# Two groups of edges a step, offsets read four at a time, and one-hot products with the table standing still

## The chip, the cores and the metric

The kernel runs on one core of one Trainium2 chip. A core has five engines with queues of their own: PE (TensorE, matrix products into PSUM), DVE (VectorE), ACT (ScalarE), POOL (GpSimd) and SP (SyncE, which here only issues transfers). The metric is device microseconds of one execution, the median of several runs.

## The reference, cut to what matters

There are 12,500 nodes with 48 features and 200,000 edges, sorted by destination. Two graph layers follow each other, and each ends in a residual sum and a layer norm:

```
x1  = layernorm(x  + segment_sum(relu([x[dst], x[src], e32] @ W1 + b1) @ W2 + b2, dst))
out = layernorm(x1 + (1 + eps) * x1 + segment_sum(relu(x1[src] + e48), dst))
```

W1 is 128 by 128 (48 rows for x[dst], 48 for x[src], 32 for the edge features), W2 is 128 by 48. All is float32. The sources are random, so x[src] and x1[src] are gathers of rows from all over the table. The destinations are sorted, so a run of 512 edges touches only a narrow window of destinations.

## The kernel before, in words

**Groups.** The edges are padded and cut into 391 groups of 512, each of four tiles of 128 edges (`TPC`, `NCHUNK`, lines 43 to 46). The nodes are cut into 14 segments of 7 blocks of 128. The destinations of a group lie in a window of 48 nodes, whose start is worked out on the chip (`base`, `off`, lines 208 to 222). `rel` holds each edge's destination less the window's start. A check on the chip (`check_windows`) lets a general path run instead if an edge falls outside; with these inputs it does not run.

**Layer 0, one group a step.** `fetch0` (399) issues four indirect DMAs on POOL, one for each tile, each gathering 128 rows of 48 values into the tile `cat`. `fill0` (404) copies the edge features into `cat` on ACT, writes the one-hot of the destination within the window on DVE, reads the group's offset into a register of SP, and lets SP load 48 rows of the projected table (`a_dram`) into one of four weight tiles `wcat`. `turn0` (414) transposes the four tiles on PE and DVE copies them to `cat_t`. `hidden0` (422) multiplies by `wcat` on PE, and ACT applies bias and relu. `message0` (429) multiplies by W2, and DVE adds b2. `sum0` (439) sums the messages by window on PE with the one-hot, and `add_window` (309) reads the offset into a register of DVE and adds the 48 by 48 result into the segment's sum.

**The order** is written out by hand (`manual_schedule`). `run` (443) goes over steps k and calls, in the order of its list, each stage for the group k less its distance: in layer 0 the fetch five groups ahead, the fill two ahead, then sum (three behind), message (two behind), hidden (one behind) and turn. Every engine works through its own instructions in this order. `finish0` (362) takes each segment's sums to x1 when its last group is through, writes x1 to HBM (`x1_dram`) and keeps x1 in SBUF as three bf16 pieces (`xp`). `project` (263) makes the table that `wcat` is loaded from.

**Layer 1.** `fetch1` (480) gathers rows of `x1_dram`, `fill1` makes the one-hot, `message1` (492) adds edge features on DVE and applies relu on ACT, and `sum1` sums as in layer 0. For 28 of the 391 groups (`PE_GROUPS`, every 13th from the 26th) no gather is issued. Their rows come from `products` (546), in batches of two groups: `place` (509) writes where in its block each source lies and turns that over on PE; for each of the 98 blocks of x1, `select` (523) makes a one-hot of 128 by 1024 on DVE in bf16, and `multiply` (528) multiplies it with the block's three pieces on PE, adding in PSUM. The one-hot stands in PE as the weight (a load for each of 8 tiles) and the pieces pass (144 columns). A `tensor_reduce` then adds the three pieces. `products` is a generator: `lead1` (580) takes one part of it, four blocks, in each step.

Of the kernel before, what the change touches and what calls it, by code (L numbers as in the profile page):

```python
# [55 lines left out]
AHEAD = 5  # L56
NW = 4
EC = 5
FIRST = 26
EVERY = 13  # L60
NPE = 28
BATCH = 2
PIECES = 3
BPS = 4

PE_GROUPS = [FIRST + EVERY * i for i in range(NPE)]
assert PE_GROUPS[-1] < NCHUNK and NPE % BATCH == 0

assert NSEG * NB == NT
STEP = CHUNK * N // E  # L70
STEP4 = 4 * CHUNK * N // E

# [56 lines left out]
def windowed(ctx, tc, dram, flag, x, src, dst, e32, e48, w1, b1, w2, b2, eps, out):  # L129
    nc = tc.nc  # L130
    const = ctx.enter_context(tc.tile_pool(name="const", bufs=1))
    onehots = ctx.enter_context(tc.tile_pool(name="onehots", bufs=2 * BPS))
    cats = ctx.enter_context(tc.tile_pool(name="cats", bufs=AHEAD + 5))
# [3 lines left out]
    node = ctx.enter_context(tc.tile_pool(name="node", bufs=2))  # L137
    psum = ctx.enter_context(tc.tile_pool(name="psum", bufs=1, space=bass.MemoryType.PSUM))
# [4 lines left out]
    dst_i = const.tile([P, NCHUNK * TPC], I32, name="dst_i")  # L143
    nc.sync.dma_start(src_i, src)
    nc.scalar.dma_start(dst_i, dst)
    seg = ctx.enter_context(tc.tile_pool(name="seg", bufs=3))
# [39 lines left out]
    lows = const.tile([1, NCHUNK], F32, name="lows")  # L186
    highs = const.tile([1, NCHUNK], F32, name="highs")
    starts = const.tile([1, NCHUNK], F32, name="starts")
    quads = -(-NCHUNK // 4)
    shares = const.tile([1, quads, 4], F32, name="shares")  # L190
# [9 lines left out]
    def gather(t, table, g, j):  # L200
# [9 lines left out]
    base = const.tile([1, NCHUNK], F32, name="base")  # L210
# [8 lines left out]
    off = const.tile([1, NCHUNK], I32, name="off")  # L219
    nc.vector.tensor_tensor(  # L220
        off, base, starts, op=ALU.subtract
# [6 lines left out]
    )  # L228

# [15 lines left out]
    part = const.tile([P, NPE, TPC], F32, name="part")  # L245
    block = const.tile([P, NPE, TPC], F32, name="block")

    def split_src():
        first = FIRST * TPC
        some = src_i[:, first : first + (NPE - 1) * EVERY * TPC].rearrange(  # L250
            "p (i c) -> p i c", c=EVERY * TPC
        )[:, :, 0:TPC]
        last = src_i[:, PE_GROUPS[-1] * TPC : (PE_GROUPS[-1] + 1) * TPC]
        bits = node.tile([P, NPE, TPC], I32, name="bits")
        for op, by, plus, to in (
            (ALU.bitwise_and, Q - 1, 0.0, part), (ALU.logical_shift_right, 7, 1.0, block)
        ):
            nc.vector.tensor_scalar(bits[:, : NPE - 1, :], some, by, None, op0=op)
            nc.vector.tensor_scalar(bits[:, NPE - 1, :], last, by, None, op0=op)
            nc.vector.tensor_scalar(to, bits, plus, None, op0=ALU.add)  # L260
# [27 lines left out]
    def load_edges(name, table, width, g):  # L288
        c = g // EC
        if g % EC == 0:  # L290
            n = min(EC, NCHUNK - g)
            chunk[name] = echunk.tile([P, EC, TPC * width], F32, name=name)
            nc.sync.dma_start(
                chunk[name][:, :n, :],
                table[g * CHUNK : (g + n) * CHUNK, :].rearrange(
                    "(c p t) d -> p c (t d)", p=P, t=TPC
                ),
            )
        return chunk[name][:, g % EC, :].rearrange("p (t d) -> p t d", t=TPC)

    def one_hot(o, g):
        nc.vector.tensor_tensor(
            o, iota_w[:, None, :].to_broadcast([P, TPC, W]),
            rel[:, g, :, None].to_broadcast([P, TPC, W]), op=ALU.is_equal,
        )

    agg = {}

    def add_window(layer, g, pa):
        s = seg_of(g)  # L310
        if (layer, s) not in agg:
            agg[layer, s] = aggs.tile([D, SROWS], F32, name="agg")
            nc.vector.memset(agg[layer, s], 0.0)
        at = nc.vector.value_load(
            off[0:1, g : g + 1], min_val=low(g) - seg_start(s), max_val=high(g) - seg_start(s)
        )
        cols = agg[layer, s][:, bass.ds(at, W)]
        nc.vector.tensor_tensor(cols, cols, pa, op=ALU.add)  # L318

    def reduce_tiles(hot, msg):  # L320
        pa = psum.tile([D, W], F32, name="pa")
        for j in range(TPC):
            nc.tensor.matmul(pa, msg[:, j, :], hot[:, j, :], start=j == 0, stop=j == TPC - 1)  # L323
# [73 lines left out]
    cat, ph, h, pm, hot = {}, {}, {}, {}, {}  # L397

    def fetch0(g):
        cat[g] = cats.tile([P, TPC, Q], F32, name="cat")  # L400
        for j in range(TPC):
            gather(cat[g][:, j, W : W + D], x, g, j)

    def fill0(g):
        e = load_edges("e32c", e32, DE, g)
        nc.scalar.activation(cat[g][:, :, W + D :], e, AF.Copy)
        one_hot(cat[g][:, :, :W], g)
        s = seg_of(g)
        at = nc.sync.value_load(
            off[0:1, g : g + 1], min_val=low(g) - seg_start(s), max_val=high(g) - seg_start(s)  # L410
        )
        nc.sync.dma_start(wcats[g % NW][0:W, :], a_dram[s][bass.ds(at, W), :])

    def turn0(g):
        pt = psum.tile([Q, TPC, P], F32, name="pt", bufs=2)
        for j in range(TPC):
            nc.tensor.transpose(pt[:, j, :], cat[g][:, j, :], ident[:P, :P])  # L417
        cat_t = work.tile([Q, TPC, P], F32, name="cat_t")
        nc.vector.tensor_copy(cat_t, pt)  # L419
        h[g] = cat_t  # L420

    def hidden0(g):
        ph = psum.tile([HID, TPC, P], F32, name="ph")
        nc.tensor.matmul(ph, wcats[g % NW], h[g], start=True, stop=True)  # L424
        t = work.tile([HID, TPC, P], F32, name="h")
        nc.scalar.activation(t, ph, AF.Relu, bias=b1_sb)  # L426
        h[g] = t

    def message0(g):
        pm = psum.tile([P, TPC, D], F32, name="pm")  # L430
        for j in range(TPC):
            nc.tensor.matmul(pm[:, j, :], h[g][:, j, :], w2_sb, start=True, stop=True)  # L432
        msg = work.tile([P, TPC, D], F32, name="msg")
        nc.vector.tensor_tensor(  # L434
            msg, pm, b2_sb[:, None, :].to_broadcast([P, TPC, D]), op=ALU.add
        )
        h[g] = msg

    def sum0(g):
        pa = reduce_tiles(cat.pop(g)[:, :, :W], h.pop(g))  # L440
        add_window(0, g, pa)

    def run(stages, finish, lead):
# [3 lines left out]
        for k in range(first, NCHUNK + last):  # L447
            for f, d in stages:
                g = k - d
                if 0 <= g < NCHUNK:  # L450
                    f(g)
                    if d == last:
                        for s in finishes.get(g, []):
                            finish(s)
            lead(k)

    def lead0(k):
        for s in range(1, NSEG):
            if k == first_group(s - 1) + 4:
                load_seg(x, s)  # L460
            if k == first_group(s - 1) + 8:
                project(s)
        if k == 14:
            check_windows()
        if k == 16:
            split_src()

    for g in range(AHEAD):
        fetch0(g)
    project(0)  # L470
    run(
        [(lambda g: g >= AHEAD and fetch0(g), -AHEAD), (fill0, -2), (sum0, 3), (message0, 2),
         (hidden0, 1), (turn0, 0)],
        finish0, lead0,
# [5 lines left out]
    def fetch1(g):  # L480
        if g in PE_GROUPS:
            return
        cat[g] = cats.tile([P, TPC, D], F32, name="xs")
        for j in range(TPC):
            gather(cat[g][:, j, :], x1_dram, g, j)

    def fill1(g):
        hot[g] = work.tile([P, TPC, W], F32, name="hot", bufs=4)
        one_hot(hot[g], g)
# [308 lines left out]
```

## Time and profile before

| what | value |
|---|---|
| median of 3 runs | 4900.48 us (4892.4 to 4907.17) |
| profiled execution, its own time | 3846.41 us |
| its span, first to last instruction | 3844.6 us |
| busy PE / PE weight loads | 2856.8 us (74%) / 2210.8 us (58%) |
| busy DVE / ACT / POOL | 1893.4 us (49%) / 564.0 us (15%) / 2887.0 us (75%) |
| mean granted PE clock | 0.787 |
| indirect DMAs on POOL | 1564 in layer 0, 1452 in layer 1 |
| PE matmul records | 23396 |

The profile is of one execution, and its durations belong to the 3846.41 us; the three runs without a profile lie 1054 us higher. Busy time counts work alone: reading registers, waiting for semaphores and issuing DMAs are not in it. "Granted clock" is the share of full speed at which PE ran. In a group's row, the name before the arrow is what is written, those after it what is read, then the shapes, the count, the busy time with the mean of one, and the engine's idle time just before these instructions.

### The profile page before, as it was taken

The page shows a single profiled execution, that of the slowest core. Times are in us where ns is not written, and L with a number is a line of the kernel's source. Part 1 is how long each engine was busy: PE and PEld are TensorE (multiplying, and loading weights), DVE is VectorE, ACT ScalarE, POOL GpSimd, SP SyncE. Part 2 cuts the span into 40 slices and gives each one's busy share as a digit, 9 for nine tenths or more (in the row PEclk, how much of TensorE's full clock was granted, in tenths as well). Part 3 has the DMA queues.
Part 4 walks back from the last instruction along what each step waited for, and adds up shares of the span by engine and source line. Part 5 has one row for each costly group of instructions (what it writes and reads, how often), then busy time and mean ns, then how long its engine had stood idle before and what let it go on. Part 6 is the DMA issues. An engine that isn't in the chain of part 4 may idle for free. (4 is left out here: it accounts for less than half of the span.)

```text
span 3844.6 us, 67581 instructions
## 1 busy us (share of the span) xinstructions
PE 2856.8 (74%) x23396; PEld 2210.8 (58%) x23396; DVE 1893.4 (49%) x4618; ACT 564.0 (15%) x1329; POOL 2887.0 (75%) x3025
## 2 busy tenths in 40 slices
PE   6888788888888888888886767667677676667731
PEld 4555555556555555556565656656566666656631
DVE  3333333333333333333356766767677676767731
ACT  2222212212212212212110000000000000000000
POOL 7777777777777777777767777777777777777776
PEclk9787877787777777777778888878887887888765
DMA  3222222222222222222222221222122222212221
GB/s 71 43 45 49 44 44 47 46 40 49 49 39 49 45 41 47 48 41 46 38 44 39 50 39 37 55 45 43 38 50 43 45 43 50 43 33 55 45 42 28
DMA packets 293005, 171.68 MB, mean 45 GB/s; under 512 B 109664, under 2 KB 292400, under 8 KB 292656
## 3 DMA queue, kind: packets, MB, share of 16 engines
q0 software_dynamic: 96512, 74.31, 13.1%
q1 hardware_dynamic: 179248, 84.31, 8.0%
q10 hardware_dynamic: 16896, 8.69, 0.7%
q8 instruction: 185, 3.03, 0.3%
q14 instruction: 164, 1.34, 0.1%
HBM read 154.45 MB, written 12.62 MB: 43 GB/s over the span
## 5 line engine op out<-in xcount | busy, mean ns | idle before, releaser
L201 POOL DMA_INDIRECT cat<-in_x_dram,src_i x1564 | 1485.1, 950 | 481.0 <-issue 339.5
L201 POOL DMA_INDIRECT xs<-x_dram,src_i x1452 | 1400.0, 964 | 461.0 <-issue 340.7
L530 PEld LDWEIGHTS <-o 128*128 128x128 bf16 x10976 | 853.0, 112 | 22.6 <-DVE o L525 0.6
L525 DVE TENSOR_SCALAR o<-pt 128x1024 bf16<-128x1024 bf16 x1372 | 848.7, 677 | 5.4 <-PE pt L520 5.4
L419 DVE COPY cat_t<-pt 128x512 f32<-128x512 f32 x391 | 270.2, 691 | 897.5 <-PE pt L417 897.5
L323 PE MATMUL pa<-hot,msg 128*48 128x48 f32 x3128 | 255.8, 234 | 561.3 <-ACT msg L497 561.2
L417 PEld LDWEIGHTS pt<-ident,cat 128*128 128x128 f32 x1564 | 265.6, 176 | 632.2 <-DMA cat<-in_x_dram,src_i 365.1
L424 PE MATMUL ph<-cat_t,wcat 128*128 128x512 f32 x782 | 580.3, 833 | 0.8 <-DVE cat_t L419 0.8
L323 PEld LDWEIGHTS pa<-hot,msg 128*48 128x48 f32 x3128 | 202.6, 144 | 642.3 <-ACT msg L497 623.1
L530 PE MATMUL ph<-xp,o 128*128 128x144 bf16 x4116 | 568.5, 256 | 0.0
L417 PE MATMUL pt<-ident,cat 128*128 128x128 f32 x1564 | 389.4, 347 | 237.2 <-DMA cat<-in_x_dram,src_i 233.9
L530 PE MATMUL pm<-xp,o 128*128 128x144 bf16 x4116 | 563.9, 254 | 0.0
L432 PE MATMUL pm<-w_sb,h 128*128 128x48 f32 x3128 | 538.0, 326 | 1.3 <-ACT h L426 1.2
L432 PEld LDWEIGHTS pm<-w_sb,h 128*128 128x128 f32 x3128 | 484.0, 236 | 27.8 <-ACT h L426 2.4
L426 ACT ACTIVATE h<-ph,b_sb 128x512 f32<-128x512 f32 x391 | 268.4, 686 | 1370.1 <-PE ph L424 1355.6
L530 PE MATMUL pt<-xp,o 128*128 128x144 bf16 x2744 | 453.8, 253 | 0.0
L495 DVE TENSOR_TENSOR m<-xs,e48c 128x192 f32<-128x192 f32 x363 | 131.4, 362 | 549.6 <-DMA xs<-x_dram,src_i 549.0
L497 ACT ACTIVATE msg<-m 128x192 f32<-128x192 f32 x391 | 141.8, 363 | 1611.9 <-DVE m L495 1611.9
L323 PE MATMUL pa<-cat,msg 128*48 128x48 f32 x3128 | 260.8, 237 | 33.4 <-DVE msg L434 25.6
L323 PEld LDWEIGHTS pa<-cat,msg 128*48 128x48 f32 x3128 | 207.8, 147 | 112.1 <-issue 52.9
L434 DVE TENSOR_TENSOR msg<-pm,b_sb 128x192 f32<-128x192 f32 x391 | 139.5, 357 | 233.6 <-PE pm L432 231.3
L318 DVE TENSOR_TENSOR agg<-agg,pa 48x48 f32 x782 | 150.3, 192 | 174.0 <-PE pa L323 122.9
(79 smaller groups left out, 1066.8 us busy)
## 6 DMA issues: line engine op xcount, KB each, us to landing
e48c<-in_e_dram SPq DMA_DIRECT2D x78, 480.0 KB
cat<-in_x_dram,src_i POOLq DMA_INDIRECT x1564
e32c<-in_e_dram SPq DMA_DIRECT2D x78, 320.0 KB
xs<-x_dram,src_i POOLq DMA_INDIRECT x1452
wcat<-a SPq DMA_DIRECT2D x391, 24.0 KB
a<-a ACTq DMA_DIRECT2D x14, 256.0 KB
a<-a ACTq DMA_DIRECT2D x14, 192.0 KB
x_seg<-in_x_dram SPq DMA_DIRECT2D x14, 168.0 KB
```

Of the source, the lines that this page charges most:

```text
L201: nc.gpsimd.indirect_dma_start(out=t, out_offset=None, in_=table, in_offset=bass.IndirectOffsetOnAxis(ap=src_i[:, g * TPC + j : g * TPC + ...
L318: nc.vector.tensor_tensor(cols, cols, pa, op=ALU.add)
L323: nc.tensor.matmul(pa, msg[:, j, :], hot[:, j, :], start=j == 0, stop=j == TPC - 1)
L417: nc.tensor.transpose(pt[:, j, :], cat[g][:, j, :], ident[:P, :P])
L419: nc.vector.tensor_copy(cat_t, pt)
L424: nc.tensor.matmul(ph, wcats[g % NW], h[g], start=True, stop=True)
L426: nc.scalar.activation(t, ph, AF.Relu, bias=b1_sb)
L432: nc.tensor.matmul(pm[:, j, :], h[g][:, j, :], w2_sb, start=True, stop=True)
L434: nc.vector.tensor_tensor(msg, pm, b2_sb[:, None, :].to_broadcast([P, TPC, D]), op=ALU.add)
L497: nc.scalar.activation(msg, m, AF.Relu)
L525: nc.vector.tensor_scalar(o, which, float(b + 1), None, op0=ALU.is_equal)
L530: nc.tensor.matmul(ps[k // PER][:, k % PER, :], o[:, k, :], xp[:, b, :, :], start=False, stop=False, skip_group_check=True,)
```

## The change

1. The unit of work becomes a pair of groups, 196 of them, the last with one group. Every instruction of a step that worked on 4 tiles works on 8: the one-hots, the copies, the relus, the b2 addition. Products on PE stay per tile or per group. The stages get closer: fetch three pairs ahead, fill one ahead, then, within a step, message of the pair before, turn of this pair, sum and add of the pair before, hidden of this pair. PSUM tiles are twice as large and single.
2. The offsets are read into registers four at a time (`start_of`), on SP and DVE each, without the range check. Edge features are loaded for six groups at once in place of five.
3. The products are for 14 pairs, which leaves out as many gathers as before. x1's pieces stand in PE (two pieces as 96 columns, the third as 48), and the one-hot of 1024 edges passes as two times 512 columns, so each block takes four matmuls in place of eight. The result comes out with features on partitions; ACT copies it to SBUF, and PE turns it back and adds the pieces by multiplying with identities (`both`, `ident`). Two parts of the generator are taken in each step, one before and one after `sum1`.
4. Tiles that only the start needs go into a pool that is closed (`early`), and the one-hots use that room.

The diff at its core:

```diff
-AHEAD = 5
+PAIRS = -(-NCHUNK // 2)
+AHEAD = 3
 NW = 4
-EC = 5
-FIRST = 26
+EC = 6
+FIRST = 14
 EVERY = 13
-NPE = 28
-BATCH = 2
+NPE = 14
 PIECES = 3
-BPS = 4
+BLOCKS = 4
...
+def groups(p):
+    return range(2 * p, min(2 * p + 2, NCHUNK))
...
-    cats = ctx.enter_context(tc.tile_pool(name="cats", bufs=AHEAD + 5))
+    cats = ctx.enter_context(tc.tile_pool(name="cats", bufs=AHEAD + 3))
...
+    def start_of(engine, layer, g):
+        if (engine, layer, g // 4) not in starts_of:
+            kind = {nc.sync: mybir.EngineType.SP, nc.vector: mybir.EngineType.DVE}[engine]
+            _, starts_of[engine, layer, g // 4] = nc.values_load_multi_w_load_instructions(
+                off[0:1, g // 4 * 4 : g // 4 * 4 + 4], engines=[kind], min_val=0,
+                max_val=SROWS - W,
+                skip_runtime_bounds_check_because="off is held to its range where it is made",
+            )
+        return starts_of[engine, layer, g // 4][g % 4]
...
-        at = nc.vector.value_load(
-            off[0:1, g : g + 1], min_val=low(g) - seg_start(s), max_val=high(g) - seg_start(s)
-        )
-        cols = agg[layer, s][:, bass.ds(at, W)]
+        cols = agg[layer, s][:, bass.ds(start_of(nc.vector, layer, g), W)]
         nc.vector.tensor_tensor(cols, cols, pa, op=ALU.add)
...
+    def turn0(p):
+        n = tiles(p)
+        pt = psum.tile([Q, 2 * TPC, P], F32, name="pt")
+        for k in range(n):
+            nc.tensor.transpose(pt[:, k, :], cat[p][:, k, :], ident[:P, :P])
+        cat_t = work.tile([Q, 2 * TPC, P], F32, name="cat_t")
+        nc.vector.tensor_copy(cat_t[:, :n, :], pt[:, :n, :])
+        h[p] = cat_t
...
     run(
-        [(lambda g: g >= AHEAD and fetch0(g), -AHEAD), (fill0, -2), (sum0, 3), (message0, 2),
-         (hidden0, 1), (turn0, 0)],
-        finish0, lead0,
+        [(lambda p: p >= AHEAD and fetch0(p), -AHEAD), (fill0, -1), (message0, 1), (turn0, 0),
+         (sum0, 1), (add0, 1), (hidden0, 0)],
+        add0, finish0, lead0,
     )
...
-    def multiply(ps, o, b):
-        for k in range(tiles):
-            nc.tensor.matmul(
-                ps[k // PER][:, k % PER, :], o[:, k, :], xp[:, b, :, :],
-                start=False, stop=False, skip_group_check=True,
-            )
+    def multiply(two, low_, o, b):
+        for t, pieces in ((two, slice(0, 2)), (low_, slice(2, 3))):
+            for a in range(2):
+                nc.tensor.matmul(
+                    t[:, a, :], xp[:, b, pieces, :].rearrange("p i d -> p (i d)"), o[:, a, :],
+                    start=b == 0, stop=b == NT - 1,
+                )
...
+            two_sb = work.tile([2 * D, 2 * TPC, P], F32, name="cat_t")
+            nc.scalar.activation(
+                two_sb.rearrange("q k e -> q (k e)"), two.rearrange("q a e -> q (a e)"), AF.Copy
+            )
+            low_sb = work.tile([D, 2 * TPC, P], F32, name="h")
+            nc.scalar.activation(
+                low_sb.rearrange("q k e -> q (k e)"), low_.rearrange("q a e -> q (a e)"), AF.Copy
+            )
+            yield
+            px = psum.tile([P, 2 * TPC, D], F32, name="pm")
+            for k in range(2 * TPC):
+                nc.tensor.matmul(px[:, k, :], two_sb[:, k, :], both, start=True, stop=False)
+                nc.tensor.matmul(
+                    px[:, k, :], low_sb[:, k, :], ident[0:D, 0:D], start=False, stop=True
+                )
+            made[p] = work.tile([P, 2 * TPC, D], F32, name="made")
+            nc.vector.tensor_copy(made[p], px)
...
-    run([(fetch1, -AHEAD), (fill1, -2), (sum1, 1), (message1, 0)], finish1, lead1)
+    run(
+        [(fetch1, -AHEAD), (fill1, -1), (message1, 0), (some_products, -AHEAD), (sum1, 0),
+         (more_products, -AHEAD), (add1, 0)],
+        add1, finish1, lead1,
+    )
```

## The prediction

> **What bounds the kernel now.** I read the page first (engine shares, then the groups), then who waited for whom on POOL, then stretches of each layer, then the order of time around the layer boundary. The waits of POOL alone, columns "us in total, times, longest":
>
> ```profile
> engine line waited for: us in total, times, longest us
> POOL xs L201 <- issue: 340.7, 1057, 18.8
> POOL cat L201 <- issue: 339.5, 1114, 0.3
> POOL xs L201 <- DMA xs<-x_dram,src_i: 86.8, 285, 0.3
> POOL cat L201 <- DMA cat<-in_x_dram,src_i: 67.7, 222, 0.3
> ```
>
> Whatever the releaser named, no pause of POOL is longer than 0.3 us, except one of 18.8 us and one of 4.6 us at the start (another line). 0.3 us is the gap between any two gathers, so it is their issue cost and no wait. The two layers' stretches, and the groups that the change touches:
>
> ```profile
> 100.00:1900.00 1800.00, 1504.72 (x8242) 1031.87 (x8240) 606.95 (x1593) 375.41 (x834) 1362.41 (x1436) 0.78 0.23 45
> 2100.00:3800.00 1700.00, 1127.21 (x13369) 1005.70 (x13369) 1135.08 (x2648) 141.79 (x389) 1291.69 (x1340) 0.80 0.22 44
> ```
>
> ```profile
> L201 POOL DMA_INDIRECT cat<-in_x_dram,src_i x1564 | 1485.1, 950 | 481.0 <-issue 339.5
> L201 POOL DMA_INDIRECT xs<-x_dram,src_i x1452 | 1400.0, 964 | 461.0 <-issue 340.7
> L525 DVE TENSOR_SCALAR o<-pt 128x1024 bf16<-128x1024 bf16 x1372 | 848.7, 677 | 5.4 <-PE pt L520 5.4
> L419 DVE COPY cat_t<-pt 128x512 f32<-128x512 f32 x391 | 270.2, 691 | 897.5 <-PE pt L417 897.5
> L495 DVE TENSOR_TENSOR m<-xs,e48c 128x192 f32<-128x192 f32 x363 | 131.4, 362 | 549.6 <-DMA xs<-x_dram,src_i 549.0
> L426 ACT ACTIVATE h<-ph,b_sb 128x512 f32<-128x512 f32 x391 | 268.4, 686 | 1370.1 <-PE ph L424 1355.6
> ```
>
> In a stretch the five busy times are PE, PEld, DVE, ACT, POOL, then the granted clock. POOL did 1436 gathers in 1800 us, one per 1.2535 us (0.95 busy + 0.30), and 1340 in 1700 us, one per 1.2687. Everyone else waits for them: DVE m 549 us for xs, the transposes for cat. So the span adds up from POOL alone: first gather at 7.2, 1564 x 1.2535 = 1960.5, the pause between the layers 18.9, 1452 x 1.2687 = 1842.1, and 17.0 from the last gather (3827.65) to the end: 3845.7 against a span of 3844.6. The execution's own time is 3846.4, 1.8 above the span.
>
> The runs shown have a median of 4900.5, 1054 us (27%) above the profiled execution. Nothing in the trace shows that excess. I sum against 3846.4 and carry the difference over; how the excess is paid is the largest unknown here.
>
> **What the Trainium skill says.** "Perfetto Trace Analysis", section "DMA Instruction — SWDGE (GPSIMD)": a gather's profile span ends when the last DSP has written its descriptors, not when data has moved. The trace agrees: starts stand 1.25 us apart with transfers in flight. So a gather costs descriptor writing, whatever the consumer does. "TensorE: Matmul & The Clock Gate", "What's actually happening": PE has two clocks, half when recent activity is low, full when high. The trace agrees: transposes start every 109 or 213 ns, and the clock falls to 0.50 in the idle last 145 us. "SBUF — State Buffer", "Who interferes with whom": DVE instructions with two SBUF inputs contend with GpSimd reads. Here gathers differ by 1.2% between the layers (1.2535, 1.2687), so this is a small term.
>
> **The change part by part.**
>
> *Gathers.* Layer 0: 391 x 4 = 1564, as before. Layer 1: 14 pairs x 8 = 112 left out, before 28 groups x 4 = 112; 1452 as before. POOL: 0 us. With 3 pairs ahead (24 gathers; before 20) and 6 pair buffers (48 gathers; before 40), a buffer is asked for when its old pair lies six back, whose sum is one step after its own: no wait.
>
> *Two groups a step, layer 0.* Sizes from rows: DVE took 1782 ns for 1564 elements and 349 for 192, so 1.044 ns an element + 149. A pair saves 149 in one-hot, msg and cat_t each: 196 x 3 x 0.149 = 88 us of DVE; in layer 1 (one-hot, m) 58 us. Worth 0, because DVE stands idle behind gathers (897.5 and 549 us). PE's products are the same: starts at full clock 112 ns (message, 16 a pair), 109 (8 transposes), 45 (16 sums), 429 (4 hidden): 1.79 + 0.87 + 0.72 + 1.72 = 5.10 us a pair; at half clock 214, 213, 80, 853: 9.82. New is waiting inside the step: before, four groups were in flight; now hidden(k) is followed at once by message(k), which waits for ACT's h of 1024 columns (686 at 512, 363 at 192: 1.01 ns an element, so 1.20) and some 0.25 of handover; and hidden waits for cat_t (691 + 512 x 1.044 = 1.23 + 0.2) behind sums of 0.72: 0.7. A step takes 5.10 + 1.45 + 0.7 = 7.25 at full clock, about 11.4 at half, against POOL's 8 x 1.2535 = 10.03. Equal rates need full clock in 24% of the time; before, it was granted for 57%. Taken: 0, hidden by POOL. If the clock stayed at half: 196 x 1.4 = +270.
>
> *Offsets four at a time.* DVE's loads fall from 782 to 196, SP's from 391 to 98. Uncounted on the page; between a one-hot's end (1003.35) and the add behind it (1003.47) lie 0.12 us, so at most 782 x 0.12 = 94 us of DVE, hidden likewise. The add behind the load now waits once in four. SP's wcat loads are issued one pair ahead (before: two groups) with the same four buffers, behind the e32 load on SP's queue and hidden(p-2): still a pair's time, 10 us, to land. 0.
>
> *Products, layer 1.* Removed: 10976 matmuls of 144 columns with 128-wide loads, which start every 62.5 ns at full clock and 120 at half, and the 84 opening and closing ones. Added: 14 x 98 x 4 = 5488 of 512 columns. No such row exists; by columns 512/144 x 62.5 = 222 ns (the skill, same page, "Wait — 56ns, not 53.3ns?", has 215.7 warm, 426.7 cold). I take 222; 427 at half. That is 1218 us in place of 686 at full clock: PE gets dearer, not cheaper, since the loads were hidden already. Per 13 pairs (one product set): 392 x 0.222 = 87.1; sums 13 x 0.72 = 9.4; back-transposes 8 x 2 x 2 x 0.112 = 3.6; finishing 1.1: 101.2 us, and about 4 idle at place. DVE: 98 x 0.677 = 66.3, place 8 x 0.243 = 1.9, one-hot and m 13 x 1.1 = 14.3, adds 5, made 0.6, finishing 5.6: 94. POOL: 12 pairs x 8 x 1.2687 = 121.8. Both fit if the mean clock is over 101.2/117.8 = 0.86. Before it was 0.80, but with PE at work half the time (60 us of 121.8 at full clock); between 2600 and 2680, in pieces of 5 us, PE busy for over 3.8 of 5 at a clock of 0.63 to 0.69 brings the clock back to 1.00 within 10 us. At 83% work I take a clock near 1. ACT gets 2 x 1.2 per set: idle. Taken: 0.
>
> *Start, boundary, end.* The last pair holds one group, so the 17 us tail and the layer boundary keep their chains; 18.9 +-2. The identity copy and its DMA (`both`) are hidden by POOL, and so is the loss of the second `pt` buffer: the next pair's transposes come a step after the copy that frees it.
>
> Sum: 3846.4 + 0 +-3; with the excess carried over, 4900.
>
> **The rivals.**
> A (forecast): POOL stays the bound, 4900, own range 4885 to 4915. For it: no POOL wait anywhere, the same 3016 gathers. Against: it supposes that the unprofiled excess is POOL's or a constant.
> B (other side): PE becomes the bound in layer 1. Its place is the 32 passes of 512 columns per step; it decides once the clock averages below 0.86. At the old 0.80 a set takes 101.2/0.80 + 4 = 130.5, 8.7 over, times 196/13: +131 us, 5031. With layer 0 also at half clock (+270) up to 5300. POOL then pauses for cats buffers.
> C: the excess of 1054 is paid per instruction outside POOL. Matmul records fall from 23396 to 23396 - 10976 - 84 + 5488 + 448 = 18272, 22%: -231, 4670; if by DVE's halved steps, down to 4400. For it: nothing else explains so large an excess; against: the profiled engines have slack everywhere.
> D: POOL's pace itself moves by up to 1% (port sharing with DVE, boundary, a missed buffer): 4850 to 4950.
>
> **How the numbers follow.** 0.3% (15 us) is about what a measurement of this kernel tells from no change. A 0.45 (within 0.38, faster 0.04, slower 0.03), B 0.32 slower, C 0.15 faster, D 0.08 (faster 0.03, slower 0.05). Faster 0.22, same 0.38, slower 0.40. The range 4840 to 5180 holds A, D and B with layer 1 alone and part of layer 0; left out are C and the top of B (0.05), together 0.20. The single likeliest case is A, so 4900.
>
> **What would show it.** Right: 3016 gathers, 0.30 before each, no longer pause than the boundary's; 512-column passes starting every 215 to 222 ns; layer 1's clock above 0.9; PE waits on ACT h of about 1.4 us a step. Wrong: POOL waiting for buffers, a layer 1 pace over 121.8 us per 13 pairs (B), or a median that moves while the profiled span does not (C).

## The result, and the profile after

| | median | range | span of the profiled execution | clock |
|---|---|---|---|---|
| before | 4903.82 us | 4892.4 to 4939.82 | (3844.6 us, the profile shown above) | 0.787 |
| after | 5114.78 us | 5095.19 to 5133.39 | 5093.4 us, own time 5095.19 | 0.774 |

The ratio is 1.0417, 95% interval 1.035 to 1.0484: slower by 211 us. The forecast was 4900 and no change.

One thing has to be known to read the numbers: the same program takes two very different times, as far as the runs go on different chips. The kernel before took 3839 to 3841 us on two chips of this study and 4837 to 4847 us on two others; which chips the recorded runs had isn't known. The recorded times (4904) are of the second kind, the profile before (3844.6) of the first. I call these the 3840 level and the 4840 level. The profile after was taken at the upper level, so it can't be laid beside the profile before line by line; the experiments do that with pairs from one chip.

The groups of the page after:

```profile
L205 POOL DMA_INDIRECT cat<-in_x_dram,src_i x1564 | 1520.4, 972 | 1000.8 <-issue 989.4
L205 POOL DMA_INDIRECT xs<-x_dram,src_i x1452 | 1411.4, 972 | 1130.2 <-DVE m L541 674.6
L581 PE MATMUL pt<-o,xp 128*96 128x512 bf16 x2744 | 940.0, 424 | 97.3 <-issue 60.3
L581 PEld LDWEIGHTS <-xp 128*96 128x96 bf16 (+1 forms) x5488 | 417.8, 115 | 1310.5 <-issue 1297.8
```

The waits of POOL after (us in total, times, longest):

```profile
POOL cat L205 <- issue: 989.4, 1542, 12.6
POOL xs L205 <- DVE m L541: 674.6, 111, 17.3
POOL xs L205 <- issue: 382.2, 1246, 1.4
```

Stretches after, one of each layer (PE, PEld, DVE, ACT, POOL, granted clock):

```profile
1000.00:1900.00 900.00, 574.43 (x3168) 421.83 (x3166) 208.58 (x395) 117.52 (x178) 534.70 (x552) 0.71 0.17 34
2700.00:3500.00 800.00, 667.36 (x3014) 246.38 (x3011) 397.07 (x785) 43.75 (x78) 440.50 (x456) 0.84 0.16 32
```

The gathers are as many as before and almost as long (972 ns against 950 and 964), but POOL now stands still between them: pauses of up to 17 us, for `m` on DVE in layer 1, whose end frees a buffer, and without a named cause in layer 0. From first to last gather layer 0 takes 2515 us and layer 1 2496. Where two gathers start over 1.5 us apart, the time beyond the usual 1.25 sums to 560 and 682 us; the profile before had 1961 and 1841 us, with 1 and 11 us of that kind. No engine is full, and the chain that ended last has moved off POOL:

```profile
PE 58%; another core or an unknown queue 21%; issue 11%; DVE 6%; ACT 4%; DMA 1%; POOL 0%; DVEq 0%; ACTq 0%; POOLq 0%
```

PE is busy for 72% of the span, so it isn't a matter of PE's work alone; the page doesn't say what else.

### The profile page after: what moved, and what is told of

It reads as the page before. It is cut to its first block, busy times and chain, and to the rows that moved or that the text cites. A ratio compares the mean times of both kernels' runs of the same rounds, so it can differ in the third digit from the quotient of the medians.

```text
span 5093.4 us, 51135 instructions
## 1 busy us (share of the span) xinstructions
PE 3674.5 (72%) x18272; PEld 1957.9 (38%) x18272; DVE 1843.0 (36%) x3616; ACT 480.1 (9%) x772; POOL 2933.7 (58%) x3025
## 4 chain that ended last, share of the span: by engine, by line
PE 58%; another core or an unknown queue 21%; issue 11%; DVE 6%; ACT 4%; DMA 1%; POOL 0%; DVEq 0%; ACTq 0%; POOLq 0%
PE pt L581 15%; PE ph L581 14%; PE ph L456 8%; PE pa L346 7%; PE pm L467 7%; PE pt L446 4%; ACT h L460 2%; DVE o L572 1%; PE pm L613 1%; DVE cat_t L448 1%; PE px L280 1%; PE pm L612 1%; DVE msg L469 1%; PE which L567 1%
## 5 line engine op out<-in xcount | busy, mean ns | idle before, releaser
L572 DVE TENSOR_SCALAR o<-which 128x1024 bf16<-128x1024 bf16 x1372 | 879.7, 681 | 519.5 <-remote 209.5
L581 PE MATMUL pt<-o,xp 128*96 128x512 bf16 x2744 | 940.0, 424 | 97.3 <-issue 60.3
L581 PE MATMUL ph<-o,xp 128*48 128x512 bf16 x2744 | 902.1, 410 | 42.1 <-issue 40.5
L581 PEld LDWEIGHTS <-xp 128*96 128x96 bf16 (+1 forms) x5488 | 417.8, 115 | 1310.5 <-issue 1297.8
L469 DVE TENSOR_TENSOR msg<-pm,b_sb 128x384 f32<-128x384 f32 x196 | 109.1, 557 | 1347.1 <-remote 520.9
L460 ACT ACTIVATE h<-ph,b_sb 128x1024 f32<-128x1024 f32 x196 | 217.7, 1111 | 1915.2 <-PE ph L456 1355.7
L448 DVE COPY cat_t<-pt 128x1024 f32<-128x1024 f32 x196 | 239.1, 1220 | 201.5 <-PE pt L446 118.9
L543 ACT ACTIVATE msg<-m 128x384 f32<-128x384 f32 x196 | 102.1, 521 | 2016.9 <-DVE m L541 1532.2
L456 PEld LDWEIGHTS ph<-cat_t,wcat 128*128 128x128 f32 x782 | 177.1, 252 | 250.1 <-issue 188.5
L313 DVE TENSOR_TENSOR cat<-iota_w,rel 128x384 f32<-128x384 f32 x196 | 109.0, 557 | 36.9 <-issue 36.5
```

Source lines behind the costliest of these rows:

```text
L313: nc.vector.tensor_tensor(o, iota_w[:, None, :].to_broadcast([P, n, W]), r[:, :, None].to_broadcast([P, n, W]), op=ALU.is_equal,)
L448: nc.vector.tensor_copy(cat_t[:, :n, :], pt[:, :n, :])
L456: nc.tensor.matmul(ph[:, part_of, :], wcats[g % NW], h[p][:, part_of, :], start=True, stop=True)
L460: nc.scalar.activation(t[:, :n, :], ph[:, :n, :], AF.Relu, bias=b1_sb)
L469: nc.vector.tensor_tensor(msg[:, :n, :], pm[:, :n, :], b2_sb[:, None, :].to_broadcast([P, n, D]), op=ALU.add)
L572: nc.vector.tensor_scalar(o.rearrange("p a e -> p (a e)"), which.rearrange("p k e -> p (k e)"), float(b + 1), None, op0=ALU.is_equal,)
```

## The experiments where the kernel before takes 3840 us

The first three runs were made for theory 1, that POOL's gathers hinder PE, against theory 2, that the excess lies outside the engines, or that PE and DVE are slow by themselves. After them came theory P: the forecast's term for the products was too small, and PE has become the bound in layer 1 (rival B's place). Its rival, theory Q, is that layer 0's shorter pipeline costs the time.

**e1: the kernel before, unchanged, and e2, e3: both kernels without gathers.** For each group (pair) one plain load of consecutive rows takes the place of the gathers, so these two kernels don't compute the right result. The edit of e2 in layer 1 (layer 0 and e3 alike):

```diff
-        for j in range(TPC):
-            gather(cat[g][:, j, :], x1_dram, g, j)
+        load_rows(cat[g], x1_dram, g, TPC)
```

> The kernel before, unchanged, profiled once more, since its first profile lasted 3846 us and its runs 4900. If its runs are slow because PE is hindered while POOL gathers (theory 1), this profile shows a span near 4900, PE matmuls of one kind with pauses while gathers are issued, and products that reach DVE and ACT more than 1 us late, as in the profile of the changed kernel. If the first profile was the usual one and the excess lies outside the engines (theory 2), the span is again near 3845 with POOL issuing a gather every 1.25 us.

> The kernel before with every gather replaced by one plain load of consecutive rows for the group, issued on SP (so the rows are not those of the sources; POOL has no work). Theory 1 (POOL's gathers hinder PE): handovers from PE are prompt, and layer 0 falls to PE's own pace, 391 groups of 2.55 us at full clock to 4.9 us at half, 1000 to 1900 us; the whole lies between 2200 and 3300 us. Theory 2 (PE and DVE are slow by themselves, whatever POOL does): the time stays above 4300 us.

> The changed kernel with every gather replaced by one plain load of consecutive rows for the pair, issued on SP (rows not those of the sources; POOL has no work). Theory 1: layer 0 takes 7.3 to 11.4 us a pair (1420 to 2230 us) in place of 12.7, layer 1 some 7.9 us a step (1550 us) in place of 13.2, and the whole 3000 to 3800 us against 5115. Theory 2: the time stays above 4500 us. If the changed kernel is still slower than the kernel before with the same loads, part of its loss is in its own chain and its dearer products.

Measured: e1 3835.64, e2 2693.75, e3 3694.17 us. The profile's 3846 is thus a time that comes again. With no excess on this chip, e1 can't decide between the two theories. Without gathers the kernel before takes 1142 us less than e1, and the changed kernel only 142 us less than e1. The busy line of e2, then of e3:

```profile
PE 2341.7 (87%) x23396; PEld 1880.9 (70%) x23396; DVE 1857.2 (69%) x4618; ACT 569.6 (21%) x1329; POOL 1.9 (0%) x9
```

```profile
PE 3170.6 (86%) x18272; PEld 1664.5 (45%) x18272; DVE 1858.5 (50%) x3616; ACT 479.5 (13%) x772; POOL 1.9 (0%) x9
```

PE is the busiest engine in both. The changed kernel takes 1000 us longer and keeps PE busy for 829 us more, although it has 22% fewer matmuls. A stretch of e3 in layer 1 has PE busy for 1657 of 1700 us at a clock of 0.95:

```profile
1900.00:3600.00 1700.00, 1657.23 (x8193) 608.53 (x8192) 1130.40 (x2147) 117.48 (x213) 0.00 (x0) 0.95 0.14 40
```

A set (the products of one pair and the 13 steps over which they are spread) took 131 to 136 us there, with POOL idle; the forecast had 101 plus about 4, and POOL needs 122.

**e4: the changed kernel; e5: the same with the old products; e6: the kernel before with the offsets read by fours.** Core of e5, which leaves pairs and offsets as they are (cuts marked by dots):

```diff
...
-                nc.tensor.matmul(
-                    t[:, a, :], xp[:, b, pieces, :].rearrange("p i d -> p (i d)"), o[:, a, :],
...
+            nc.tensor.matmul(
+                ps[k // PER][:, k % PER, :], o[:, k, :], xp[:, b, :, :],
...
```

> The changed kernel, unchanged, where the kernel before takes 3840 us. If the loss is the dearer products (theory P: a block's four matmuls start over 1.10 us, so a set of 13 steps needs 126 us of PE against 122 us of POOL), layer 0 runs at POOL's pace (about 1970 us), layer 1 at PE's, 10.1 to 10.6 us a step (1980 to 2080 us), and the whole takes 3960 to 4080 us. If the loss is layer 0's shorter pipeline (theory Q), layer 0 alone is over 2150 us and layer 1 about 1860. If everything waits for POOL as the prediction had it, 3840.

> The changed kernel with the products of the kernel before put back: one-hot standing, x1's pieces passing in 144 columns, a reduction in place of the turn back. Theory P: layer 1 returns to POOL's pace, 121.8 us for 13 steps, and the whole is within 0.5% of the kernel before. Theory Q: it stays as slow as the changed kernel, within 1%.

> The kernel before with offsets read four at a time and nothing else. Theories P and Q alike: the reads are hidden behind POOL, so within 0.3% of the kernel before. If DVE's register reads were on the path, 1 to 2% faster.

Measured against the kernel before on the same chip (3840.72):

| run | us | ratio | 95% |
|---|---|---|---|
| e4, whole change | 3985.22 | 1.0379 | 1.036 to 1.0397 |
| e5, pairs and offsets, old products | 3854.31 | 1.0034 | 1.0021 to 1.0047 |
| e6, offsets alone | 3840.36 | 0.9999 | 0.9991 to 1.0008 |

So at this level the loss is in the new products, 131 of 145 us, and it lies in layer 1, with sets of 131 to 136 us as in e3, where there are no gathers: 1972.4 us from first to last gather in e4 against 1832.8 in e1, while layer 0 has 1964.8 against 1960.0. The stretch 2100 to 3700 of e1, then of e4:

```profile
2100.00:3700.00 1600.00, 1098.01 (x13201) 981.50 (x13199) 1113.42 (x2572) 133.76 (x367) 1214.19 (x1267) 0.82 0.23 44
```

```profile
2100.00:3700.00 1600.00, 1557.92 (x7709) 574.43 (x7707) 1060.56 (x2016) 111.49 (x201) 1196.98 (x1176) 0.95 0.21 40
```

PE has gone from 69% to 97% busy. The clock rose to 0.95, so it isn't the low clock that rival B named. In e4's groups the weight loads have lost time:

```profile
L572 DVE TENSOR_SCALAR o<-which 128x1024 bf16<-128x1024 bf16 x1372 | 919.8, 688 | 347.6 <-PE ph L581 341.3
L581 PEld LDWEIGHTS <-xp 128*96 128x96 bf16 (+1 forms) x5488 | 399.0, 112 | 1073.0 <-issue 1061.2
```

and its timeline of the weight loads shows how (start us, length us, in brackets the idle time before):

```profile
3003.90 0.17 PEld L581 LDWEIGHTS <-xp 128*96 128x96 bf16 x2
3004.47 0.12 PEld L581 LDWEIGHTS <-xp 128*48 128x48 bf16 x2 [0.40 <-issue]
3005.01 0.17 PEld L581 LDWEIGHTS <-xp 128*96 128x96 bf16 x2 [0.42 <-issue]
3005.57 0.12 PEld L581 LDWEIGHTS <-xp 128*48 128x48 bf16 x2 [0.40 <-issue]
```

Each time the width of the weights changes, from 96 columns to 48 or back, the load stands idle for 0.4 us. The starts of the matmuls in e4 at full clock (medians over the trace): 253 ns within the 96 columns, 233 within the 48, and 309 at each change. A block of four takes 253 + 309 + 233 + 309 = 1104 ns in place of 4 x 222 = 888.

**e7: old products, pairs, but 17 pairs made on PE in place of 14** (every 11th, five blocks a part; 24 gathers fewer than before), as a version that uses what PE has left.

> As the one with old products, but 17 pairs made on PE (every 11th step, five blocks in each part) in place of 14: 24 gathers fewer, 30 us of POOL. Theory P with POOL as the bound again: 0.8% faster than the kernel before. If DVE, then at some 89 us of 101 for 11 steps, or PE sets the pace instead: no faster or slower.

Measured: 3830.31, ratio 0.9977 (0.9968 to 0.9986). It beats both kernels at this level, by less than expected: 24 gathers are 30 us, of which the cost of the pairs (e5: 14 us) comes off, and some 6 us more. In e5 and e7 two gathers start 1.5 to 2.2 us apart more often (41 and 49 times in layer 1, against 9 in e1). The gathers themselves get longer: in layer 1 of e4 the 156 that share 0.7 us or more with DVE's tensor_tensor instructions (mostly a pair's one-hot and `m`) last 1.55 us on average, and the 1051 that share nothing with them 0.945. The Trainium skill ("SBUF — State Buffer", "Who interferes with whom") says that DVE instructions with two SBUF inputs contend with GpSimd's reads. Layer 1 of e4 agrees; in its layer 0 the 282 gathers that share 0.4 to 0.7 us last 0.965, and no run separates this from the rest of the pairs' 14 us.

**e8, e9, e10: is it the length of PE's set, and is it the width?** Theory P: PE's set of 126 us (with the measured starts) no longer fits under POOL's 121.8. Rival H: fixed hitches at each hand-over from one-hot to product. e8 spreads a set over 14 steps, e9 leaves out the third piece, and e10 makes the two weights equally wide:

```diff
-        for t, pieces in ((two, slice(0, 2)), (low_, slice(2, 3))):
+        for t, pieces in ((two, slice(0, 2)), (low_, slice(1, 3))):
```

> The changed kernel with 13 pairs made on PE, every 14th, in place of 14, every 13th: a set of products is spread over 14 steps, nothing else changes, and POOL has 8 gathers more (1460 in layer 1). Theory P (a set is PE's own work and is too long for its 13 steps: 98 blocks x 1.103 us + 9.4 of sums + 3.6 of turning back + 1.1 of finishing + 4 of placing = 126 us, against 12 pairs x 8 x 1.27 = 121.8 of gathers): with 13 pairs to gather POOL needs 132 and PE 127, so POOL sets the pace again, layer 1 takes 1460 x 1.2705 = 1855 in place of 1972, and the time falls from 3985 to about 3868. Rival H (each set costs a fixed 10 us of hitches, 139.6 / 14, at the hand-overs between the one-hots and their products, however much time there is): 1855 + 13 x 10, about 3995.

> The changed kernel with the third piece of x1 left out of the products (the rows of the 14 pairs lose their last bits): two matmuls a block in place of four, the same one-hots on DVE, the same gathers. Theory P: the remaining two take 506 ns a block, a set some 68 us, and POOL sets the pace: layer 1 about 1845, the time about 3858. Rival H (the hand-overs of the one-hots, or DVE's instructions that slow POOL's gathers): nothing changes on that side, 3985.

> The changed kernel with the second and third piece standing in PE for the second pair of matmuls (96 columns) in place of the third alone (48 columns); what the second piece adds there is multiplied by zero in the turn back, so the result is the same sum. The number of matmuls and their 512 columns stay. Theory W (the 309 ns from one tile's matmuls to the other's, against 253 and 232 within one, come from the change of width between 96 and 48 columns): all four take 253, a block 1.012 us, a set 117 us, and POOL sets the pace again, 3860 to 3875. Theory N (the 309 ns come with any other weights, whatever their width): 2 x 309 + 2 x 253 = 1.124 us a block, a set 128 us, layer 1 up by 15 x 2, about 4010.

Measured against 3841.28: e8 3925.48, ratio 1.0221 (1.0204 to 1.0238); e9 3852.23, 1.0028 (1.0018 to 1.0038); e10 3852.63, 1.0031 (1.0021 to 1.0042).

e10 has as many matmuls as e4 and more weight columns, and it takes back the whole loss beyond what the pairs cost (e5: 1.0034). Its weight loads no longer pause. Two groups and one line of the timeline of e10:

```profile
L584 PEld LDWEIGHTS <-xp 128*96 128x96 bf16 x5488 | 677.5, 126 | 513.7 <-issue 46.6
L575 DVE TENSOR_SCALAR o<-which 128x1024 bf16<-128x1024 bf16 x1372 | 848.2, 682 | 26.0 <-PE ph L584 19.7
```

```profile
3003.38 2.54 PEld L584 LDWEIGHTS <-xp 128*96 128x96 bf16 x13
```

The idle time put down to issue falls from 1061 to 47 us, and DVE's wait for the products from 341 to 20. All four starts are 216 ns, also from one tile to the other. Theory W had expected 253, since I took 253 for the pace inside one width; it is the change that lengthens the starts around it too. e9 also has 216 ns.

e8 fell less than theory P said: 57 us are missing. Its trace has a set every 135.6 us where 127 were expected, still more than the 132 that POOL needs for 13 pairs, and 13 x 3.5 = 46 us of the 57. The term that was too small is the turn from one set to the next. From the last product of a set to the first of the next lie 15.3 us in e8 and 13.3 in e4, where the forecast's turn back, finishing and place add up to 3.6 + 1.1 + 4 = 8.7; part of the turn back runs at half clock (in e4 starts 0.29 us apart in place of 0.18). So H is out (by e9, for which it said 3985), and P holds with a longer set.

## The experiments where the kernel before takes 4840 us

The next runs fell on chips of the other level, on which the recorded comparison stands. They showed that the width of the weights isn't the main cause of the recorded loss.

**e11, e12 and e16: the kernel before, single groups and old products, with 34 or 36 groups made on PE** in place of 28, meant as a better version.

> The kernel before with its own products and single groups, but every 11th group made on PE, 34 in place of 28, five blocks a step in place of four: 24 gathers fewer. If POOL's gathers are the whole bound in it and the products of 144 columns still fit (a set of two groups in 22 steps; POOL needs 20 x 4 x 1.2687 = 101.5 us for these, DVE by the measured share 66.3 for one-hots and 0.57 a step, 79): 24 x 1.2687 = 30 us less, 3840 to 3810, ratio 0.992. Rival: PE's or DVE's share of a set no longer fits, as it didn't in the changed kernel, and the time stays at 3840 or above.

> The same further on: every 10th group, 36 of them, six blocks a step, 32 gathers fewer. POOL needs 18 x 4 x 1.2687 = 91.4 us for a set's steps, DVE 66.3 + 20 x 0.57 = 78. If it still fits: 32 x 1.2687 = 41 us less, about 3800, ratio 0.989. Rival, as for the 34: DVE or PE sets the pace (a step with six one-hots holds 4.1 + 0.9 us of DVE against 5.07 of POOL) and less than half of it arrives: over 3820.

> The kernel before with 34 groups made on PE in place of 28, as in e11 (1.0115 where the kernel before took 4843). Where the kernel before takes 3840: POOL's gathers are the bound there, 24 fewer x 1.2687 = 30 us, 3810, ratio 0.992; if the products no longer fit into their 22 steps, 1.00 or more.

Measured: e11 4900.95, ratio 1.0115 (1.0075 to 1.0155) against 4842.57; e12 4954.44, 1.024 (1.0202 to 1.0277); e16 4892.46, 1.0128 (1.01 to 1.0156) against 4837.47. Fewer gathers, more time: at this level POOL's gathers aren't the bound of the kernel before, and more work on PE and DVE costs. What they would do at 3840 stays open.

**e13, e14, e15: the kernels of e10, e5 and e2 again**, that is the whole change with equal widths, pairs with the old products, and the kernel before without gathers.

> The changed kernel with the second and third piece (96 columns) in the second pair of matmuls, as in e10. Where the kernel before takes 3840: 3853 again. Where it takes 4840 to 4900: if the change of width makes the recorded loss, 1.0417 falls to within 1.00 to 1.015; if that loss has another cause at this level (PE slowed by something else, so that each instruction or each set costs), it stays at 1.03 or above.

> The changed kernel with the products of the kernel before, as in e5. Where the kernel before takes 3840: 3854 again, and level with e13. Where it takes 4840 to 4900: if the steps of two groups alone cost there as little as elsewhere (1.0034), 1.00 to 1.01; if the longer chain within a step (turn, hidden, message) is no longer hidden there, 1.02 to 1.04.

> The kernel before with each group's gathers replaced by one plain load of consecutive rows, as in e2 (the rows are not those of the sources). If the level of 4840 to 4900 comes from POOL's gathers acting on the other engines, it takes 2694 wherever it runs. If PE or the chip as a whole is slower there, it takes 27% more there, some 3400.

| run, against 4837.47 | us | ratio | 95% |
|---|---|---|---|
| e14, pairs and offsets, old products | 5088.58 | 1.0535 | 1.0497 to 1.0573 |
| e13, whole change, equal widths | 4999.57 | 1.0337 | 1.0306 to 1.0367 |
| (recorded, whole change, against 4903.82) | 5114.78 | 1.0417 | 1.035 to 1.0484 |
| e15, before without gathers | 2706.35 | 0.5599 | 0.558 to 0.5619 |

Three things follow. First, without gathers the kernel before takes the same time at both levels (2706 and 2694): neither PE nor the chip as a whole is slower; the 1000 us come only while POOL gathers. Secondly, the pairs, which cost 0.34% at 3840, cost 5.35% here, more than the whole recorded loss and more than either case of e14's expectation had. Thirdly, the new products with equal widths take some of it back, 89 us in e13. What the change of width costs here isn't told: 1.0417 against 1.0337 is 0.8%, across two occasions and with intervals that overlap. The recorded loss comes from the two groups a step with what goes with them: e14 also has the offsets read by fours (0.9999 alone at 3840, not tried alone here), and its PSUM tiles are single. What I had shown at 3840 is at most a small part of it.

By parts (start of the first to start of the last gather, from the traces of e14 and e16, whose layer 0 is that of the kernel before): layer 0 2491.6 against 2443.4, +48; boundary 45.8 against 36.4, +9; end 16.2 against 32.6, -16; the rest of the 251 us, +210, is put down to layer 1, since no trace of the kernel before itself was kept at this level.

What is different at this level? The starts of gathers still have a median of 1.249 us, and gathers land as soon after their start as at the other level (median 2.12 us in e14 and e16, 2.11 in the profile before). But results are taken up late. Lateness of a hand-over here is the start of the receiving instruction, less the later of the end of PE's last instruction on that tile and the end of the working instruction before it on its engine; sum over those above 0.5 us, and how many:

```
                                before (3844.6)   e16        e14        after
PE pa -> DVE agg, of 782          0.5 (1)      630 (250)  551 (186)  727 (230)
PE pt -> DVE cat_t, of 391 / 196  0 (0)        455 (156)  117 (46)    76 (36)
PE pm -> DVE msg, of 391 / 196    0 (0)        379 (154)  306 (65)   337 (64)
PE ph -> ACT h, of 391 / 196      0 (0)        458 (131)  136 (64)   167 (75)
```

ACT is as late as DVE. What is late is PE's signal. PE counts up a semaphore when a product is done, and the traces record the steps of that count: in 665 of the 691 late hand-overs of e16, 351 of 361 in e14 and 397 of 405 after, a step is recorded within 0.2 us before the receiver starts. At this level 14 to 19% of the steps follow each other by 25 to 50 ns, as if they had queued; in the profile before none do. A hand-over in which PE has no part is prompt: of 391 from DVE's `m` to ACT in e16 none is over 0.12 us late. PE's own start is late as well: its weight loads for the sum begin more than 0.5 us after ACT's `msg` and PE's last load 237 times in e16 (of 3128), 14 times in the profile before.

These traces lack records, so their named releasers are to be taken with care: e16 has 16,503 events of DMA landings where the profile before has 58,357 for nearly the same transfers, and 2713 of 3329 steps of PE's count. e15, on the same chip without gathers, lacks none of PE's. That the recording itself holds the signals back is a rival that no experiment here tests; the three runs of the kernel before that are said to be without a profile took 4900, which speaks against it.

Pairs have fewer hand-overs and, with the new products, fewer PE instructions, so less lateness in sum; the reading that they have less other work under way to hide it I tested with the last two runs.

**e17: pairs with the sum a step later; e18: the kernel before with the sum in the same step as its message**, which shortens the distance of dependent work in layer 1 and changes nothing else.

```diff
-    run([(fetch1, -AHEAD), (fill1, -2), (sum1, 1), (message1, 0)], finish1, lead1)
+    run([(fetch1, -AHEAD), (fill1, -2), (message1, 0), (sum1, 0)], finish1, lead1)
```

> The pairs with the products of the kernel before (as e14), but in layer 1 the sum and its add are those of the pair before, and stand ahead of this pair's message, as in the kernel before; one more buffer for the one-hots. Where the kernel before takes 4840: if the chain within a step (message on DVE and ACT, then the sum on PE, then the add on DVE, all in one step) is what the pairs cost in layer 1, most of its 210 us go, 5089 to about 4900, ratio 1.01 to 1.02; if pairs cost as such (waits twice as long because a step is twice as large), it stays above 1.045. Where the kernel before takes 3840: POOL's gathers hide both, 3854 as in e5, or up to 8 us less.

> The kernel before with, in layer 1, the sum of a group right behind its message in the same step, in place of one step later; nothing else changes. Where the kernel before takes 4840: if the chain within a step is the cause, layer 1 grows by some 200 us, ratio about 1.04; if not, within 1.01. Where the kernel before takes 3840: a step has 5.07 us of gathers to hide it, within 1.003.

Measured against 4846.66: e17 5152.84, ratio 1.0639 (1.0594 to 1.0683); e18 5080.84, 1.0489 (1.0449 to 1.0529).

e18 says that the order alone, without pairs, can cost about as much at this level as the pairs did; it wasn't run at 3840. Waits in the stretch 2600 to 4800 of e16 (sum a step later, as in the kernel before), then of e18:

```profile
DVE agg L318 <- remote: 403.5, 102, 7.0
PE pa L323 <- ACT msg L497: 55.6, 45, 4.7
```

```profile
DVE agg L318 <- remote: 689.6, 120, 8.2
PE pa L323 <- ACT msg L497: 523.7, 223, 8.5
```

PE now waits for the message, DVE for the sum ("remote": a step of a semaphore ended the wait, and no instruction that makes it had ended within 1.5 us before), and the next one-hots and the next `m` stand behind that on DVE. e18's timeline (start us, length us) shows one such wait:

```profile
3005.04 0.38 PE L323 MATMUL pa<-hot,msg 128*48 128x48 f32 x2 [0.47 <-issue]
...
3006.45 0.52 PE L530 MATMUL ph<-xp,o 128*128 128x144 bf16 x3 [1.03 <-issue]
...
3006.51 0.95 POOL L201 DMA_INDIRECT xs<-x_dram,src_i  x1 [0.30 <-issue]
3007.18 0.28 PE L530 MATMUL pm<-xp,o 128*128 128x144 bf16 x1 [0.21 <-issue]
...
3008.58 0.40 PE L530 MATMUL pm<-xp,o 128*128 128x144 bf16 x2 [1.12 <-issue]
...
3009.29 0.53 PE L530 MATMUL ph<-xp,o 128*128 128x144 bf16 x3
3009.50 0.20 DVE L318 TENSOR_TENSOR agg<-agg,pa 48x48 f32 x1 [7.00 <-remote]
...
3012.89 0.95 POOL L201 DMA_INDIRECT xs<-x_dram,src_i  x1 [5.43 <-DVE m L495]
```

The sum is through at 3005.42; the step of PE's count for it is recorded at 3009.47, and DVE starts its add at 3009.50. Meanwhile PE goes on in strides of about 0.70 us, with one to three matmuls at each. The last gather of a run begins at 3006.51 and ends at 3007.46; within a microsecond of the time at which its data should have landed (start plus 2.1), both PE and DVE go on without pauses, and POOL then stands for 5.43 us because `m` is late. Such stretches repeat through the trace, but the end of a run of gathers isn't what always ends them: two thirds of e18's 742 late hand-overs are taken up less than 2 us after a gather's start.

e17 went the other way than expected: the longer distance did not help the pairs, they lost about another 1% (e14 and e17 on two chips of this level). It isn't a clean counterpart of e18, though. To put the sum first I moved `m` behind four one-hots on DVE, which wait for PE, and `m` is what frees POOL's buffers. The waits of POOL for `m` (2600 to 4800) go from 565.7 us in e14 to 678.5 in e17, and the longest from 15.3 to 22.1. So that dependent distance matters at this level is shown on single groups; which step of the pairs costs the 210 us in layer 1, and how much of it is the chain within a step, stays open.

Open too is why two of four chips hold PE and its signals back while POOL gathers. Gathers take part in it (e15), transfers aren't slower, and signals of DVE to ACT aren't late; more the runs don't show.

## Why the prediction was wrong, point by point

- **"Two groups a step ... Taken: 0, hidden by POOL": the step that failed.** The mechanism was written down ("New is waiting inside the step"), and the size was right where the profile was taken: PE's wait for `h` in e4 is 271.4 us over 196 steps, 1.4 a step as forecast, layer 0 has 1964.8 us against 1960.0, and pairs and offsets cost +0.34%. At the recorded level they cost +5.35%, 251 us (e14). There POOL no longer hides the waiting, since hand-overs from PE of 0.04 us become ones of several us. That a step has no second or third group to fill them is the likely reason, shown for single groups by e18 and not for pairs (e17).
- **"The excess carried over" made it wrong by so much.** The forecast named an excess of 1054 us that nothing in the trace showed as the largest unknown, and then took it as a constant. It is there only under gathers (e15), it comes with late hand-overs (the table above; that they make up all of it isn't shown), and it grows with the order of the work (e18). A profile of 3846 beside runs of 4900 was a profile of another situation, and POOL's not waiting in it said nothing about the runs.
- **Products: 222 ns a matmul.** Right for equal widths: 216 ns in e9 and e10 (the Trainium skill's 215.7, "TensorE: Matmul & The Clock Gate", "Wait — 56ns, not 53.3ns?", agrees). Wrong for this kernel: with 96 and 48 columns in turn the mean is 276 ns, 98 x 1.104 = 108 us a set in place of 87. With sums of 9.4 and the turn between sets (13.3 in place of 8.7) that makes 131 us, and 131 to 136 were measured, against POOL's 121.8. "Since the loads were hidden already" was the wrong inference: loads of one width are hidden, a change of width isn't. At 3840 this makes 131 of the 145 us; at the recorded level its share isn't told from nothing.
- **Rival B** had the right place at 3840, PE in layer 1, and the wrong cause: it decided below a mean clock of 0.86, and the clock was 0.95. Its layer 0 at half clock did not come there; in the recorded profile the clock in layer 0 is 0.71, with PE busy for 64% of the stretch.
- **Rival C**, the excess paid outside POOL: right that fewer gathers don't lessen it (e11, e12), right in sign for the products of equal width (5088.58 to 4999.57 at the same gathers), and by far too large at -231 us; the pairs were expected to gain by it and lost.
- **Offsets: 0.** 0.9999 at 3840; not tried alone at 4840. **Gathers, boundary, end:** 3016 gathers and the layers' ends as said at 3840 (in e4 a pause of 19.4 us between the layers, tail 15.8). The forecast's own tail of 17.0 was read 1 us too long: the last gather before starts at 3828.77, 15.8 before the end.
- **Rival D**, POOL's pace: +0.3% with the pairs at 3840, within its 1%.

## What to carry to other kernels

When the times shown and the profile disagree by a quarter, the profile's slack isn't slack: price every longer dependent chain as if it were exposed, and keep several independent pieces of work in flight (shown here for single groups, e18). Price a matmul together with the load of its weights, and keep standing weights equally wide, even if part of the columns is then computed for nothing (133 us here at the lower level, 3985.22 to 3852.63). An edit that exchanges many short instructions for few long ones should be measured apart from one that merges steps; here, at the 4840 level, the two had opposite signs (e14, e13).

## What the hardware showed that was not expected

- Alternating weights of 96 and 48 columns under 512-column matmuls: 309 ns at each change and 253 and 233 ns within, against 216 ns throughout with 96 everywhere.
- The same program, 3839 to 3841 us on two chips and 4837 to 4847 on two others; without GpSimd's gathers 2694 and 2706.
- Under the gathers of the upper level, hand-overs from PE to DVE of up to 12 us in place of 0.04 (e16, `pt` to `cat_t`), to ACT alike, with PE's semaphore steps recorded just before they end; from DVE to ACT none. In such a stretch PE moves in strides of 0.70 us.
- Gathers of 1.55 us on average in place of 0.945 where they share 0.7 us or more with DVE's tensor_tensor instructions (e4, layer 1).
